# Graph message passing on one core: gathers released by message products, one wait for a quad's four one-hot columns, and bases loaded for eight quads at once

## The chip, the cores and the metric

The kernel runs on one core of one Trainium2 chip. The metric is the device time of one execution in microseconds (us), shown as the median of several runs. One more execution is taken by the hardware profiler; its time stands beside its span, which is the time from the first to the last instruction. Engines are called by the names of the profile: PE is TensorE (matmul), DVE is VectorE, ACT is ScalarE, POOL is GpSimd and SP is SyncE; "PEld" is TensorE's weight load, and an engine's name with a "q" (DVEq) is its sequencer or its DMA queue.

## What is computed

400,000 edges, sorted by destination, carry messages between 12,500 nodes of 128 features; a small network of each edge's length weighs the message, the sums per destination go through two layers, and a layer norm closes it:

```python
rbf = exp(-(distances[:, None] - centers) ** 2 / (2.0 * width * width))        # 50 centers from 0 to 10
cut = 0.5 * (cos(pi * distances / CUTOFF) + 1.0) * (distances <= CUTOFF)       # CUTOFF = 10
W = (silu(rbf @ fw1 + fb1) @ fw2 + fb2) * cut[:, None]
messages = (h[src] @ pw + pb) * W
agg = segment_sum(messages, dst, num_segments=12500)
x = layernorm(x + h + (silu(agg @ mw1 + mb1) @ mw2 + mb2))                     # here h is x
```

Lengths run up to 56, so that an edge over 10 (cut is 0) adds nothing, and fewer than a fifth of the edges count.

## The kernel before

**Packing.** The edges come in seven chunks. For each chunk the kernel works out which edges are within the cutoff and packs their source, destination, length and cut closely together. The pieces of this packing (DVE, PE and a scatter on POOL's queue at L524) are put between the steps of the main loop; the last chunk is packed in the second half of the run.

**Table.** In the first 118 us PE also multiplies x by pw and adds pb; the result, `proj`, lies in DRAM, one row per node.

**Main loop.** The packed edges are taken in quads of 4 x 128 edges, 139 in all (q = 0 to 138). For each quad:

- `fetch` gathers 4 x 128 rows of `proj` with four indirect DMAs on POOL's queue (L1099), one of 21 buffers a quad, later fewer. All the buffers are named by what they are lent from: the tiles `quad`, and `x`.
- `basis` (ACT), `first` (PE, L1167, tile `ph`), `silu` (ACT, L1173) and `second` (PE, L1182 and L1185, a PSUM `bank`) work out W without the cut.
- `message` is one DVE product of 128 x 512: the gathered rows by that bank (L1201). It writes `msg`, or, from quad 66 on, in half of the quads, a buffer called `quad`.
- `place` writes the quad's four one-hot columns (DVE, L1214, tile `hot`, or `quad` in half of the quads from 66 on): column j has the cut of an edge at the place of its destination within a window, 56 to 128 wide. These operations are called columns below.
- `sum_up` multiplies on PE: four products msg^T x hot, each in two passes (L1235, PSUM tile `sums`).
- `add` adds the window to the table of all sums `aggT` on DVE (L1269). Where the window begins is a number in memory (`base_i`); DVE's sequencer loads it into a register, for two quads at a time in `bases_of` (L1244) or for one in `base_of` (L1255). From quad 69 on a quad has two windows and so two bases.

In the loop the order of a quad is: `message(q)`, parts of the packing and of the node layer, the gathers that are due, `second(q+2)`, `first` and `silu` of another pair of quads, `sum_up(q)`, loads of bases, `place(q+1)`, and `add` of the two quads before. From quad 70 on the node layer (L1283 and the lines behind it) begins for the rows of `aggT` that are complete.

**Buffers.** `msg` and `hot` have two buffers each before quad 66 and four from then on, so `place(q+1)` writes into the buffer that the products of quad q-1 read: until those are through, the column has to wait.

**When a gather goes.** A table written out by hand, `PACE`, says at which count of DVE instructions (of the kinds in `VECTORS`) a gather is to go; `pace(q, j)` interpolates in it. `gathers` puts a gather on POOL's queue once that many DVE instructions have been written, and `fetch` adds a dependency: the gather waits for exactly that DVE instruction.

```python
    while queue and (queue[0][0] < must or len(vectors) >= pace(*queue[0])):
        ...
            g.ins, vectors[min(pace(q, j), len(vectors)) - 1],
```

The instructions of one engine run in the order in which they are written. The waits are semaphores that a framework puts in from what each instruction reads and writes. In the rows of instructions below, `PE_49`, `DVE_49` and so on are the semaphores that the named engine counts up, `DMASW0_49` to `DMASW7_49` those of POOL's DMAs.

Of the kernel before, what the change touches and what calls it, by code (L numbers as in the profile page):

```python
# [16 lines left out]
OP = mybir.AluOpType  # L17
# [9 lines left out]
W = 128  # L27
WIDE_0 = 128
WIDTHS = (56, 56, 80, 112, 80, 104, 128)
QT = 4  # L30
# [9 lines left out]
QB = (0, 13, 24, 46, 69, 91, 114, 141)  # L40
# [3 lines left out]
NL = 139  # L44
# [13 lines left out]
DIRECT = 32  # L58
FIRST = 16
LISTS = 5  # L60
PACE = ((2, 17), (3, 26), (4, 36), (5, 54), (7, 95), (9, 125), (10, 144), (12, 170), (18, 250), (24, 324), (30, 373), (36, 458), (42, 544), (48, 612), (54, 691), (60, 754), (66, 826), (72, 902), (78, 982), (84, 1071), (90, 1139), (96, 1218), (102, 1306), (108, 1357), (114, 1414), (120, 1461), (126, 1518), (132, 1580), (138, 1646), (139, 1666))
VECTORS = ("TensorScalarPtr", "TensorTensor", "CopyPredicated", "TensorReduce", "TensorCopy",
           "BNStats")
SPILL = 4
# [27 lines left out]
def kernel(  # L92
# [37 lines left out]
    nc = tc.nc  # L130
# [14 lines left out]
    keep = ctx.enter_context(tc.tile_pool(name="keep", bufs=1))  # L145
# [291 lines left out]

        return max((m for m in range(q) if place_of(m) == place_of(q)), default=-1)

    vectors, queue = [], []  # L440

    def logged(i):

# [5 lines left out]
    def pace(q, j):  # L449

        (a, u), (b, v) = next((k for k in zip(PACE, PACE[1:]) if q < k[1][0]))
        n = int(u + (v - u) * (q + j / QT - a) / (b - a))
        return n - sum(1 for w in WERE if w < q - 2)

    def gathers(must=0):

        while queue and (queue[0][0] < must or len(vectors) >= pace(*queue[0])):
            q, j = queue.pop(0)
            fetch(q, js=(j,))

    def room(q):

# [369 lines left out]
    def unpack(c):  # L832
# [66 lines left out]
        def back(t):  # L899
            held.remove(c)  # L900
            free.append(t)
# [19 lines left out]
        def to_places(f, to):  # L921
            t, tp = turned()
            for j in range(2):
                nc.tensor.transpose(tp[:, j, :np_], f[:, j * P:(j + 1) * P], ident[:np_, :np_])
            if to is srci:
                lengths()
                yield 1.4 if c < 2 else 0.8
            if to is dl:
                nc.tensor.matmul(tp[0:1, 0, P:P + np_], base, ident[:np_, :np_], start=True, stop=True)
            yield later(-2.0 if c == 1 and to is srci else 0.0)  # L930
            nc.vector.tensor_copy(to[:, p0:p0 + np_, :].rearrange("p r j -> p j r"),
                                  tp[:, :, :np_])
            if to is dl:
                nc.vector.tensor_copy(base_i[:, p0:p0 + np_], tp[0:1, 0, P:P + np_])
            back(t)

        yield from to_places(f_src, srci)
# [102 lines left out]
            own_sb[name, k] = keep.tile([P, QT, H], F32, name=f"{name}{k}")  # L1040
        return own_sb[name, k]

    own_sb = {}
# [49 lines left out]
    def fetch(q, idx=None, table=None, js=range(QT)):  # L1093
        got = quad_sb[place_of(q) if q >= 0 else 0]
        for j in js:
            if q in SINGLY and j == 0:
                continue
            i = srci[:, 2 * q + j // 2, j % 2:j % 2 + 1] if idx is None else idx[:, j:j + 1]
            g = nc.gpsimd.indirect_dma_start(  # L1099
                out=got[:, j, :], out_offset=None, in_=proj if table is None else table,  # L1100
                in_offset=bass.IndirectOffsetOnAxis(ap=i, axis=0))
            if PACE[0][0] <= q < NL:
                tc.add_manual_dep(
                    g.ins, vectors[min(pace(q, j), len(vectors)) - 1],
                    mybir.DependencyInfo(mybir.DependencyClass.Sync, mybir.DependencyReason.DATA))
        got_of[q] = got

# [81 lines left out]
    def message(q, js=(0, QT)):  # L1189
        gathers(q + 1)  # L1190
        msg = own(q, "msg", 0)
        a, b = js
        if q in SINGLY and a == 0:
            act = q in BY_ACT
            k = (BY_ACT if act else BY_SP).index(q)
            assert q in alone and all(s[0] != q for s in singles[act])
            nc.vector.wait_ge(row_sem[act][k % ROW_SEMS], 16 * P * (k // ROW_SEMS + 1))
            m = nc.vector.tensor_mul(msg[:, 0, :], pu_of[q][:, :H], alone.pop(q))
            tc.declare_no_dep(m.ins, group="rows", reason="waits on row_sem")
            a = 1  # L1200
        nc.vector.tensor_mul(msg[:, a:b, :], pu_of[q].rearrange("p (j f) -> p j f", j=QT)[:, a:b, :],  # L1201
                             got_of[q][:, a:b, :])
        if b == QT:
            free.append(pu_of.pop(q))
            got_of.pop(q)
        gathers()
        return msg

    def place(q):

        hot = own(q, "hot", 1)
        for j in range(QT):
            at = 2 * q + j // 2, slice(j % 2, j % 2 + 1)
            nc.vector.tensor_scalar(hot[:, j, :wide(q)], iota_n[:, :wide(q)], dl[:, at[0], at[1]],  # L1214
                                    cut[:, at[0], at[1]], op0=OP.is_equal, op1=OP.mult)
            gathers()
        hot_of[q] = hot

    def wide(q):

        return WIDE_0 if q < DIRECT // QT else WIDTHS[chunk_of(q)]

    def windows(q):

        return 1 if chunk_of(q) < WIDE_C else 2

    def sum_up(q, msg, js=range(QT)):
        hot = hot_of[q]
        if q % 2 == 0 and 0 in js:
            pa_of["two"] = ps.tile([P, 2, 2 * W], F32, name="sums", bufs=2)  # L1230
        pa = pa_of[q] = pa_of["two"][:, q % 2, :]
        n = QT // windows(q)
        for j in js:
            k = j // n
            nc.tensor.matmul(pa[:, k * W:k * W + wide(q)], msg[:, j, :], hot[:, j, :wide(q)],  # L1235
                             start=(j % n == 0), stop=(j % n == n - 1))

    bases = {}

    def bases_of(quads_now):  # L1240

# [9 lines left out]
    def base_of(q, ks=(0, 1)):  # L1251
        for k in ks:
            if k == windows(q):
                break
            _, v = nc.values_load_multi_w_load_instructions(  # L1255
                base_i[0:1, 2 * q + k:2 * q + k + 1], engines=[mybir.EngineType.DVE],
                min_val=0, max_val=N - wide(q),
                skip_runtime_bounds_check_because="bases are destinations, and end in the table")
            bases[q, k] = v[0]
# [333 lines left out]
    for q in range(NL - 7):  # L1593
        while todo and q + 2 >= DIRECT // QT and todo[0] <= chunk_of(min(q + 2, NQ - 1)):
            go_on(todo[0])
        msg = message(q)
        nodes(q)
        most[0] = room(q)
        fetches(clock[0], most[0])
        fetches(math.inf, min(NL, q + AHEAD + 1))  # L1600
        gathers()
        assert fetched[0] > QT * min(NL - 1, q + AHEAD)
        if q >= CLEAR_Q:
            clear()
        if loads_later and q >= 8:
            nc.sync.dma_start(*loads_later.pop(0))
        radials(q // 2 + 5)
        one_by_one()
        multiplies(q + 1 + EARLY_X)
        if q + 2 < NL:  # L1610
            second(q + 2)
        if q % 4 < 2 and 2 * octs(q) < NL:
            first(octs(q))
            silu(octs(q))
        if q % 4 == 3:
            for o in (q // 4 * 2 + 4, q // 4 * 2 + 5):
# [278 lines left out]
```

## Time and profile before

| | before |
|---|---|
| runs | 941.9, 945.89 and 944.31 us, median 944.31 |
| profiled execution | 950.38 us, span 948.8 us |
| mean granted TensorE clock | 0.808 |
| PE busy | 663.7 us (70%), 3531 instructions |
| PEld busy | 517.3 us (55%), 3531 |
| DVE busy | 565.9 us (60%), 1725 |
| ACT busy | 398.0 us (42%), 567 |
| POOL busy | 539.2 us (57%), 577 |

The busy time of an engine is the sum over its instructions, so none of the engines is busy all the time. Where the profile says `A <- B`, an instruction A of this engine stood idle until B released it; "remote" is a semaphore that came without a cause in the profile's records of that time, "issue" is idle time in which the engine waited for nothing that the profile shows.

### The profile page before, as it was taken

Reading aid. Unit: us, or ns where it says so; the run is one execution under the profiler, and the core shown is the slowest. Engines: PE = TensorE matmul, PEld = TensorE weight load, DVE = VectorE, ACT = ScalarE, POOL = GpSimd, SP = SyncE. Lnnn points to the kernel's source line nnn. Section 1 sums busy time; section 2 is a strip of 40 time slices with the busy share of each in tenths; the row PEclk is TensorE's granted clock in tenths of the full one; section 3 lists DMA queues with packets and bytes.
Section 4 is the critical chain, followed back from the end, with each engine's and each line's share of the span. In section 5 each row is a group of like instructions: output and inputs, shape, how many; then the busy total and the mean of one; then the engine's idle time right before and its main releaser. Section 6 shows DMA issues by size and latency. Waiting matters only on the chain.

```text
span 948.8 us, 11718 instructions
## 1 busy us (share of the span) xinstructions
PE 663.7 (70%) x3531; PEld 517.3 (55%) x3531; DVE 565.9 (60%) x1725; ACT 398.0 (42%) x567; POOL 539.2 (57%) x577
## 2 busy tenths in 40 slices
PE   4663737749778867767767786868796675777656
PEld 3552535537556755655555564646575554554444
DVE  8356638745778767767678584646553344443536
ACT  4432622316335443534334433634643542454235
POOL 6346355565556656666666465546565566664661
PEclk8677767778778878888978898769987787778778
DMA  7574421232233223232324122432422342232222
GB/s 243 161 222 154 147 96 34 77 92 81 62 79 120 71 62 82 69 108 77 94 64 136 54 68 67 120 100 67 142 63 63 105 122 67 65 111 81 70 75 74
DMA packets 51295, 91.23 MB, mean 96 GB/s; under 512 B 12928, under 2 KB 18656, under 8 KB 51226
## 3 DMA queue, kind: packets, MB, share of 16 engines
q0 software_dynamic: 18096, 37.30, 15.6%
q1 hardware_dynamic: 22868, 35.09, 11.2%
q10 hardware_dynamic: 10262, 18.05, 6.0%
q8 instruction: 29, 0.48, 0.2%
q14 instruction: 40, 0.33, 0.1%
HBM read 74.59 MB, written 15.79 MB: 95 GB/s over the span
## 4 chain that ended last, share of the span: by engine, by line
PE 42%; another core or an unknown queue 16%; issue 13%; DVE 13%; ACT 10%; DVEq 1%; DMA 1%; ACTq 0%
PE ph L1167 11%; PE bank L1185 9%; PE sums L1235 9%; PE bank L348 5%; DVE hot L1214 3%; PE bank L1182 3%; PE bank L1283 2%; DVE msg L1201 2%; ACT s L1173 2%; ACT rbf L1151 2%; PE bank L1003 1%; PE bank L345 1%; ACT rbf L1155 1%; DVE aggT L1269 1%
## 5 line engine op out<-in xcount | busy, mean ns | idle before, releaser
L1099 POOL DMA_INDIRECT quad<-proj,srci x412 | 391.7, 951 | 274.0 <-issue 86.1
L1185 PEld LDWEIGHTS bank<-fw_sb,s 128*128 128x128 f32 x1112 | 177.1, 225 | 90.2 <-issue 83.6
L1173 ACT ACTIVATE s<-ph 128x1024 f32<-128x1024 f32 x70 | 71.2, 1017 | 335.6 <-PE ph L1167 159.9
L1167 PE MATMUL ph<-rbf,w_sb 102*128 102x512 f32 x278 | 164.1, 719 | 51.7 <-ACT s L1173 35.7
L1185 PE MATMUL bank<-fw_sb,s 128*128 128x128 f32 x1112 | 180.1, 310 | 22.5 <-issue 22.2
L1214 DVE TENSOR_SCALAR hot<-iota_n,dl,cut 128x80 f32<-128x80 f32 (+4 forms) x408 | 111.1, 338 | 107.0 <-PE sums L1235 49.6
L1235 PEld LDWEIGHTS sums<-hot,msg 128*128 128x128 f32 x816 | 121.5, 218 | 61.3 <-issue 40.3
L1235 PE MATMUL sums<-hot,msg 128*128 128x80 f32 (+4 forms) x816 | 122.5, 299 | 17.3 <-DVE msg L1201 10.1
L1099 POOL DMA_INDIRECT x<-proj,srci x96 | 91.4, 952 | 66.4 <-issue 21.3
L1167 PEld LDWEIGHTS ph<-rbf,w_sb 102*128 102x128 f32 x278 | 57.3, 229 | 99.7 <-issue 58.8
L1269 DVE TENSOR_TENSOR aggT<-aggT,sums 128x80 f32 (+4 forms) x209 | 53.9, 258 | 94.1 <-remote 33.8
L1182 PE MATMUL bank<-fb_b,ones_b 96*128 96x512 bf16 x139 | 60.3, 434 | 49.6 <-DVE msg L1201 15.2
L1201 DVE TENSOR_TENSOR msg<-bank,quad 128x512 f32<-128x512 f32 x78 | 53.2, 682 | 46.2 <-remote 32.7
L348 PEld LDWEIGHTS bank<-pw_sb,xT 128*128 128x128 f32 (+1 forms) x292 | 47.2, 232 | 59.0 <-issue 40.3
L1099 POOL DMA_INDIRECT quad<-in_x_dram,srci x48 | 46.3, 965 | 33.9 <-issue 12.6
L1235 PE MATMUL sums<-quad,quad 128*128 128x128 f32 (+3 forms) x296 | 49.4, 309 | 15.8 <-issue 15.2
L1151 ACT ACTIVATE rbf<-d_sb,rbf_bias,rbf_scale 102x512 f32<-102x512 f32 x70 | 56.1, 801 | 0.0
L1235 PEld LDWEIGHTS sums<-quad,quad 128*128 128x128 f32 x296 | 45.0, 225 | 20.1 <-issue 18.8
L348 PE MATMUL bank<-pw_sb,xT 128*128 128x128 f32 (+1 forms) x292 | 48.5, 319 | 6.2 <-ACT xT L1005 5.6
L345 PE MATMUL bank<-pb_b,ones_b 96*128 96x512 bf16 (+2 forms) x38 | 16.8, 443 | 46.4 <-ACT xT L1005 29.0
L1201 DVE TENSOR_TENSOR quad<-bank,quad 128x512 f32<-128x512 f32 (+1 forms) x40 | 25.9, 647 | 38.0 <-DMA quad<-proj,srci 24.2
L1005 ACT COPY xT<-bank 128x512 f32<-128x512 f32 (+1 forms) x37 | 21.3, 580 | 63.5 <-remote 49.0
(278 smaller groups left out, 881.7 us busy)
## 6 DMA issues: line engine op xcount, KB each, us to landing
d_sb<-near_d ACTq DMA_DIRECT2D x67, 256.0 KB
x<-in_x_dram SPq DMA_DIRECT2D x46, 256.0 KB
quad<-proj,srci POOLq DMA_INDIRECT x412
proj<-hp SPq DMA_DIRECT2D x24, 256.0 KB
out_dram<-x SPq DMA_DIRECT2D x22, 256.0 KB
x<-proj,srci POOLq DMA_INDIRECT x96
r_d<-in_edge_weight_dram SPq DMA_DIRECT2D x5, 256.0 KB
r_dst<-in_dst_dram SPq DMA_DIRECT2D x5, 256.0 KB
```

What stands on the lines that cost most here:

```text
L345: nc.tensor.matmul(to[:m, a:a + c, :], ones_b[:, :m], bias_b[:, :c, :], start=True, stop=False)
L348: nc.tensor.matmul(to[:m, k, :], lT[:, k * P:k * P + m], w, start=False, stop=(k == a + c - 1))
L1099: g = nc.gpsimd.indirect_dma_start(out=got[:, j, :], out_offset=None, in_=proj if table is None else table, in_offset=bass.IndirectOffsetO ...
L1151: a = nc.scalar.activation(rbf[:u], d[:u], AF.Square, bias=rbf_bias[:u], scale=rbf_scale[:u])
L1167: nc.tensor.matmul(ph[:, h, :], w1_sb[:2 * KR, h, :], rbf[:2 * KR], start=True, stop=True)
L1173: nc.scalar.activation(s[:, :n], ph[:, :n], AF.Silu)
L1182: nc.tensor.matmul(pu, ones_b[:, :P], bias_b["fb2"].rearrange("k j f -> k (j f)"), start=True, stop=False)
L1185: nc.tensor.matmul(pu[:, j * H:(j + 1) * H], s[:, j * P:(j + 1) * P], fw2_sb, start=False, stop=(j == QT - 1))
L1201: nc.vector.tensor_mul(msg[:, a:b, :], pu_of[q].rearrange("p (j f) -> p j f", j=QT)[:, a:b, :], got_of[q][:, a:b, :])
L1214: nc.vector.tensor_scalar(hot[:, j, :wide(q)], iota_n[:, :wide(q)], dl[:, at[0], at[1]], cut[:, at[0], at[1]], op0=OP.is_equal, op1=OP.mult)
L1235: nc.tensor.matmul(pa[:, k * W:k * W + wide(q)], msg[:, j, :], hot[:, j, :wide(q)], start=(j % n == 0), stop=(j % n == n - 1))
L1269: nc.vector.tensor_add(to, to, pa[:, k * W:k * W + wide(q)])
```

## The change

It has three parts. Gathers: `products` keeps the count of DVE instructions at each message product. A gather is put on the queue at the first message product whose count is at least its pace less `HALF` (6), at the latest when the pace plus 6 is reached, and waits for that message product in place of any DVE instruction. Columns: of a quad's four columns only the first has a dependency on the products that read the buffer before, and it is on the last of them; the other three have none. Bases: `bases_of` loads up to eight quads' bases in one instruction, as far as the windows are of one width and number and their bases are there; what is loaded isn't loaded again.

```diff
+HALF = 6
+BASES = 8
 def gathers(must=0):
-        while queue and (queue[0][0] < must or len(vectors) >= pace(*queue[0])):
+        while queue and (queue[0][0] < must or products[-1:] >= [pace(*queue[0]) - HALF]
+                         or len(vectors) >= pace(*queue[0]) + HALF):
             q, j = queue.pop(0)
             fetch(q, js=(j,))
+    def tied_to(q, j):
+        n = pace(q, j) - HALF
+        return vectors[next((k for k in products if k >= n), products[-1]) - 1]
...
             if to is dl:
                 nc.vector.tensor_copy(base_i[:, p0:p0 + np_], tp[0:1, 0, P:P + np_])
+                with_base[0] = QB[c + 1]
...
-            if PACE[0][0] <= q < NL:
+            if PACE[0][0] <= q < NL and products:
                 tc.add_manual_dep(
-                    g.ins, vectors[min(pace(q, j), len(vectors)) - 1],
+                    g.ins, tied_to(q, j),
...
             got_of.pop(q)
+            products.append(len(vectors))
...
-            nc.vector.tensor_scalar(hot[:, j, :wide(q)], iota_n[:, :wide(q)], dl[:, at[0], at[1]],
-                                    cut[:, at[0], at[1]], op0=OP.is_equal, op1=OP.mult)
+            i = nc.vector.tensor_scalar(hot[:, j, :wide(q)], iota_n[:, :wide(q)], dl[:, at[0], at[1]],
+                                        cut[:, at[0], at[1]], op0=OP.is_equal, op1=OP.mult).ins
+            if id(hot) in read_by:
+                tc.declare_no_dep(i, group="sums", keep=[read_by[id(hot)]] if j == 0 else [],
+                                  reason="a quad's first column waits for the last product")
+                if j == 0:
+                    tc.add_manual_dep(i, read_by[id(hot)].name, mybir.DependencyInfo(
+                        mybir.DependencyClass.Sync, mybir.DependencyReason.DATA))
...
-            nc.tensor.matmul(pa[:, k * W:k * W + wide(q)], msg[:, j, :], hot[:, j, :wide(q)],
-                             start=(j % n == 0), stop=(j % n == n - 1))
+            i = nc.tensor.matmul(pa[:, k * W:k * W + wide(q)], msg[:, j, :], hot[:, j, :wide(q)],
+                                 start=(j % n == 0), stop=(j % n == n - 1)).ins
+            if not tc.in_control_flow:
+                tc.add_to_no_dep_group("sums", i)
+                read_by[id(hot)] = i
...
             if k == windows(q):
                 break
+            if (q, k) in bases:
+                continue
...
         if at_once:
-            bases_of(list(now))
+            ahead = list(now)
+            while (len(ahead) < BASES and ahead[-1] + 1 < min(with_base[0], NL - 7)
+                   and wide(ahead[-1] + 1) == wide(now[0])
+                   and windows(ahead[-1] + 1) == windows(now[0])):
+                ahead.append(ahead[-1] + 1)
+            if any((k, 0) not in bases for k in now):
+                bases_of([k for k in ahead if (k, 0) not in bases])
```

What this does to the engines' instructions is seen at two places. The first is DVE around quads 14 and 15, before:

```order
L1201 TENSOR_TENSOR msg0_1078<-bank0_167,x41_87 128x512 [waits DMASW4_49,DMASW5_49,DMASW3_49,DMASW2_49]
L1214 TENSOR_SCALAR hot1_1111<-iota_n_145,dl_158,cut_157 128x56 [waits PE_49] x4
L931 COPY cut_157<-bank2_169 128x2x44
L549 SCALAR_TENSOR_TENSOR nodes_1783<-bank3_170,nodes_1729 128x512 [waits DVE_49]
L1201 TENSOR_TENSOR msg1_680<-bank1_168,x42_88 128x512 [waits DMASW6_49,DMASW7_49,DMASW1_49,DMASW0_49]
L1244 TENSOR_LOAD base_i_159 [waits DVE_49]
L1214 TENSOR_SCALAR hot0_1073<-iota_n_145,dl_158,cut_157 128x56 [waits PE_49] x4
L1269 ISA
L1269 TENSOR_TENSOR aggT_99<-aggT_99,sums_1715 128x56
```

The same place on DVE in the changed kernel (its line numbers are higher by some 10 to 20):

```order
L1210 TENSOR_TENSOR msg0_1078<-bank0_167,x41_87 128x512 [waits DMASW4_49,DMASW5_49,DMASW3_49,DMASW2_49]
L1224 TENSOR_SCALAR hot1_1111<-iota_n_145,dl_158,cut_157 128x56 [waits PE_49]
L1224 TENSOR_SCALAR hot1_1111<-iota_n_145,dl_158,cut_157 128x56 x3
L939 COPY cut_157<-bank2_169 128x2x44
L557 SCALAR_TENSOR_TENSOR nodes_1787<-bank3_170,nodes_1738 128x512 [waits DVE_49]
L1210 TENSOR_TENSOR msg1_680<-bank1_168,x42_88 128x512 [waits DMASW6_49,DMASW7_49,DMASW1_49,DMASW0_49]
L1224 TENSOR_SCALAR hot0_1073<-iota_n_145,dl_158,cut_157 128x56 [waits PE_49]
L1224 TENSOR_SCALAR hot0_1073<-iota_n_145,dl_158,cut_157 128x56 x3
L1290 ISA
L1290 TENSOR_TENSOR aggT_99<-aggT_99,sums_1724 128x56
```

The order is the same; three of four columns have lost their wait on PE, and the load of bases between product and columns is gone here (quad 11 has loaded those of quads 8 to 15). From quad 66 on no column waits for PE in either kernel. Over the whole program DVE has 24 loads of bases in place of 82, with 1 to 16 registers each, and 62 columns wait on PE in place of 248; the instructions of PE that count a semaphore up fall from 601 to 393.

The second place is POOL's queue at the gathers of quads 113 and 114, before:

```order
L1099 DMA quad9_82<-proj,srci_156 128x128 [waits DMASW3_49,DVE_49]
L1099 DMA quad9_82<-proj,srci_156 128x128 [waits DMASW4_49,DVE_49]
L1099 DMA quad9_82<-proj,srci_156 128x128 [waits DMASW5_49,DVE_49]
L1099 DMA quad9_82<-proj,srci_156 128x128 [waits DMASW6_49,DVE_49]
L1099 DMA quad10_83<-proj,srci_156 128x128 [waits DMASW7_49,DVE_49]
L1099 DMA quad10_83<-proj,srci_156 128x128 [waits DMASW0_49,DVE_49]
L1099 DMA quad10_83<-proj,srci_156 128x128 [waits DMASW1_49,DVE_49]
L1099 DMA quad10_83<-proj,srci_156 128x128 [waits DMASW2_49,DVE_49]
```

The same gathers in the changed kernel:

```order
L1108 DMA quad9_82<-proj,srci_156 128x128 [waits DMASW3_49]
L1108 DMA quad9_82<-proj,srci_156 128x128 [waits DMASW4_49]
L1108 DMA quad9_82<-proj,srci_156 128x128 [waits DMASW5_49,DVE_49]
L1108 DMA quad9_82<-proj,srci_156 128x128 [waits DMASW6_49]
L1108 DMA quad10_83<-proj,srci_156 128x128 [waits DMASW7_49]
L1108 DMA quad10_83<-proj,srci_156 128x128 [waits DMASW0_49]
L1108 DMA quad10_83<-proj,srci_156 128x128 [waits DMASW1_49,DVE_49]
L1108 DMA quad10_83<-proj,srci_156 128x128 [waits DMASW2_49]
```

Before, each gather waits for a DVE instruction of its own; now the third of a quad's gathers waits for a message product here, and the next three go with it. The gathers' own order is kept; only beside the scatters of L524 a few of them change places by one to three.

More of the change, by code (lines that the diff above doesn't have):

```diff
@@ L438, in before_it @@
         return max((m for m in range(q) if place_of(m) == place_of(q)), default=-1)
-    vectors, queue = [], []
+    vectors, queue, products = [], [], []
     def logged(i):
@@ L1041, in own @@
         return own_sb[name, k]
-    own_sb = {}
+    own_sb, read_by = {}, {}
     singles, alone, regs, row_at = ([], []), {}, {}, [0.0]
@@ L1234, in sum_up @@
             k = j // n
-            nc.tensor.matmul(pa[:, k * W:k * W + wide(q)], msg[:, j, :], hot[:, j, :wide(q)],
-                             start=(j % n == 0), stop=(j % n == n - 1))
-    bases = {}
+            i = nc.tensor.matmul(pa[:, k * W:k * W + wide(q)], msg[:, j, :], hot[:, j, :wide(q)],
[3 more added lines that the diff above has]
+                read_by[id(hot)] = i
+    bases, with_base = {}, [DIRECT // QT]
     def bases_of(quads_now):
```

## The prediction

> **What bounds the kernel now.** I read the page first, for a leader among the engines.
>
> ```profile
> span 948.8 us, 11718 instructions
> ...
> PE 663.7 (70%) x3531; PEld 517.3 (55%) x3531; DVE 565.9 (60%) x1725; ACT 398.0 (42%) x567; POOL 539.2 (57%) x577
> ...
> PE 42%; another core or an unknown queue 16%; issue 13%; DVE 13%; ACT 10%; DVEq 1%; DMA 1%; ACTq 0%
> ```
>
> None is above 70%, and the chain that ended last is mostly PE; its second share, 16% or 152 us, is signals that came late without a recorded cause. On one core "another core" can only be a queue or a semaphore that was slow. So each stage has to be read by who waits in it. The windows cut the run at quad 66 (499 us), from which columns no longer wait for PE, and at 700 us.
>
> ```profile
> core 0: us, PE busy (x) PEld busy (x) DVE busy (x) ACT busy (x) POOL busy (x), PEclk, DMA share, GB/s
> 130.00:499.00 369.00, 266.63 (x1388) 209.21 (x1388) 251.45 (x677) 143.55 (x178) 219.10 (x231) 0.80 0.28 76
> 499.00:700.00 201.00, 154.53 (x832) 117.92 (x831) 120.78 (x402) 95.14 (x133) 114.01 (x120) 0.85 0.33 93
> 700.00:949.00 249.00, 171.68 (x895) 130.48 (x894) 114.06 (x392) 105.07 (x159) 138.28 (x147) 0.81 0.28 82
> ```
>
> DVE is busy 68% of the first of these stretches and 46% of the last. Its waits in 130 to 499 us, and then in 499 to 949 us:
>
> ```profile
> DVE hot L1214 <- PE sums L1235: 49.6, 18, 14.6
> DVE hot L1214 <- remote: 44.9, 18, 5.3
> ...
> DVE aggT L1269 <- remote: 33.8, 7, 6.7
> DVE msg L1201 <- remote: 30.9, 5, 8.3
> DVE quad L1201 <- DMA quad<-proj,srci: 24.2, 10, 4.8
> DVE quad L1201 <- remote: 10.0, 3, 6.2
> DVE msg L1201 <- DMA quad<-proj,srci: 7.8, 4, 2.3
> ```
>
> In the first stretch 94.5 of DVE's 117.6 idle us stand ahead of the columns: the change touches the very wait that holds DVE there. In the second it touches only the gathers, which hold a message 14 times, 32.0 us together.
>
> **The columns.** Two kinds of waits are in those 94.5 us; DVE's timeline shows both.
>
> ```profile
> 429.94 1.08 DVE L1214 TENSOR_SCALAR hot<-iota_n,dl,cut 128x112 f32<-128x112 f32 x4 [3.75 <-remote]
> ...
> 171.35 0.34 DVE L1214 TENSOR_SCALAR hot<-iota_n,dl,cut 128x128 f32<-128x128 f32 x1 [0.35 <-PE bank L1003]
> ...
> 466.86 0.34 DVE L1214 TENSOR_SCALAR hot<-iota_n,dl,cut 128x112 f32<-128x112 f32 x1 [1.63 <-PE sums L1235]
> 468.96 0.34 DVE L1214 TENSOR_SCALAR hot<-iota_n,dl,cut 128x112 f32<-128x112 f32 x1 [1.76 <-remote]
> 471.06 0.34 DVE L1214 TENSOR_SCALAR hot<-iota_n,dl,cut 128x112 f32<-128x112 f32 x1 [1.76 <-remote]
> 471.79 0.34 DVE L1214 TENSOR_SCALAR hot<-iota_n,dl,cut 128x112 f32<-128x112 f32 x1 [0.40 <-remote]
> ```
>
> In the first row all four columns run in one piece: (1.08 - 0.34) / 3 = 0.25 us from one start to the next. There are 19 such places up to 499 us. The last product's signal was there at most 3 x 0.25 = 0.74 us after the first one's, or the fourth column would have stood alone. Waiting for it at the first column therefore costs 0 to 0.74 us, together 0 to 14.
>
> In ten other quads the signals came one by one: 17 rows like the last three, from 171.35 to 471.79 us, show 18.8 us of idle time between a quad's columns. Now the first column starts when the last signal comes, where the fourth starts today, and the other three follow: if the last signal comes as now, each of the ten loses 0.74 us, 7.4 together. If it comes as early as the first one does now, all 18.8 us are gone. So the columns are worth -18.8 to +21.4.
>
> Which? The steps in the last four rows are 2.10, 2.10 and 0.73 us, though the products themselves are short:
>
> ```profile
> L1235 PE MATMUL sums<-hot,msg x816: 209/275/554, 145.4 to 936.3; 128*128 128x80 f32 x52, 128*128 128x112 f32 x34, 128*128 128x128 f32 x33, 128*128 128x56 f32 x26
> L1235 PE MATMUL sums<-quad,quad x296: 229/275/539, 506.1 to 939.8; 128*128 128x128 f32 x52, 128*128 128x80 f32 x44, 128*128 128x104 f32 x44, 128*128 128x112 f32 x8
> ```
>
> By PE's records the products were over long before ("remote"), so signals are late, which speaks for a gain by fewer of them. Against it: "remote" waits do not thin out from 499 us on, where no column waits for PE (33.8 + 30.9 + 10.0 us there in three rows alone, 44.9 at the columns before). The rows point both ways between ends that lie almost evenly about nothing; I take 0 and keep both ends. What hides a small loss here is the next late signal of PE: DVE comes to it 0.7 us later and waits 0.7 us less.
>
> [...]
>
> Behind the first column stand, on DVE, the other three, the two sums into aggT, the packing's steps and the next message product; for that product's `msg` and these columns wait PE's next products, and now also the gathers tied to it. All of it moves by what the column moves.
>
> **The gathers.** POOL's rows:
>
> ```profile
> L1099 POOL DMA_INDIRECT quad<-proj,srci x412: 938/944/1322, 104.7 to 930.2; - x138
> ...
> 708.64 0.94 POOL L1099 DMA_INDIRECT quad<-proj,srci  x1 [0.30 <-issue]
> 709.89 0.94 POOL L1099 DMA_INDIRECT quad<-proj,srci  x1 [0.30 <-issue]
> ```
>
> A gather holds POOL 0.944 us and the next starts 0.30 us behind it, although each has a wait on DVE of its own; 1.25 us each, 5.0 us for four. Taking waits away makes this no shorter: nothing. What moves is when a gather may start. The four of a quad were released over the quad's 9 to 15 DVE instructions; now about four are released at one message product, some earlier than their count and some later (the tie is the first product from count - 6 on). For a mean distance of 12 between products that is 6 earlier to 6 later, on average nothing; but four released together run 5.0 us, so the last of them starts 3.75 us behind its release.
>
> Before 499 us DVE never waits for a gather (no such row), so nothing comes of it there. Behind 700 us it does. I replayed POOL's queue with DVE's times held: each gather starts at the later of its new release plus the usual 0.3 us and the end of the gather ahead plus 0.30. Late gathers come 0.5 to 1 us later on average, two quads (105 and 117) nearly 5, with their messages 1.6 and 1.9 us later; over the waits for gathers that is about +3.5 us. It could also be -2 (gathers released earlier that today wait for their count) or +10 (the same delay at each of the 14 waits). Behind 700 us a message that is late is partly covered by late PE work: I take +2.
>
> **The loads of bases.** They run in DVE's sequencer, between product and columns.
>
> ```profile
> L1244 DVEq TENSOR_LOAD <-base_i x32: 508/512/757, 161.0 to 497.4; - x32
> L1244 DVEq TENSOR_LOAD <-base_i x28: 337/344/686, 509.4 to 845.5; - x28
> L1244 DVEq TENSOR_LOAD <-base_i x1: 1333/1333/1333, 901.3 to 901.3; - x1
> L1201 DVE TENSOR_TENSOR msg<-bank,quad x78: 665/681/698, 120.9 to 934.1; 128x512 f32<-128x512 f32 x78
> 902.71 1.12 DVE L1214 TENSOR_SCALAR hot<-iota_n,dl,cut 128x128 f32<-128x128 f32 x4 [0.57 <-issue]
>   issue: 5.9, 10
> ```
>
> The three groups are loads of 2 registers with a stride, of 4 in a row and one of 14 in a row. The message product of 0.68 us covers loads of 0.51 and 0.34 us; columns stand idle by "issue" 5.9 us in the whole run (last row, of the view of L1214), 0.57 of it behind the one load that is longer than a product, of 14 registers. So removing 58 loads saves at most 5.9 - 0.57 = 5.3 us, likely 3.5. The new ones are longer: 16 registers in a row take about 1.33 + 2 x (1.33 - 0.34) / 10 = 1.5 us and stick out 0.85 us; 8 with a stride 0.51 + 6 x 0.10 = 1.1 to 4 x 0.51 = 2.0 us, 0.4 to 1.4 beyond the product. Eight strided and seven or so long ones cost 9 to 17 us if nothing covered them; the strided ones lie ahead of columns that wait for PE in 29 quads of 64 anyway. From -5 to +12; I take -1.
>
> **Columns beside gathers.** A gather released by the message product starts on top of the columns that follow.
>
> ```profile
> L1214 DVE TENSOR_SCALAR hot<-iota_n,dl,cut x408: 275/328/569, 117.8 to 931.8; 128x80 f32<-128x80 f32 x44, 128x112 f32<-128x112 f32 x28, 128x128 f32<-128x128 f32 x27, 128x56 f32<-128x56 f32 x21
> ```
>
> The longest column is 0.24 us over the median; today some columns end beside a gather and are held by up to that. If one more column in 20 to 60 quads is held by 0.1 us or less, that is 0 to +5 us on DVE, less on the path; I take 0.
>
> **Sum:** 0 + 2 - 1 + 0 = +1 us on the profiled execution's 950.38. That execution lies 6.1 us above the median of the runs (944.31), so I forecast 945.3, said as 945.
>
> **Rivals.** What this kernel can tell from no change is about 0.5%, 4.7 us: 939.6 to 949.0.
>
> *A, late signals are PE's own making (faster).* If fewer signals let the last one come where the first comes now, the ten trickling quads give back up to 18.8 us, and a part of the 44.9 us of "remote" goes too. For it: the 2.10 us steps while PE's records have moved on. Against it: the "remote" rows from 499 us on. With two thirds of the 18.8 on the path, 933.
>
> *B, pacing or loads help (faster).* POOL idles until a DVE instruction of its own count; earlier releases take some of that away, and 58 loads less take away 5.3 us. With -2 for gathers and -5 for loads, 938.
>
> *C, the last product costs (slower).* If signals come as now, the 29 quads lose 7.4 + up to 14 us, of which DVE's chain before 499 us passes most on: it decides when DVE rather than PE is late at the columns. With two thirds of 21, +14: 958. It decides from about 0.3 us a quad on.
>
> *D, bursts are late behind 700 us (slower).* If each of the 14 gather-bound messages loses 0.6 to 0.7 us and a few more join them, +9: 953.
>
> *E, an engine blocks the other (slower).* If columns and gathers that now start together excluded each other, each of some 120 quads would lose up to a column, 0.33 us, or +40: 984. The row above speaks against it, since no column is held longer than 0.24 us and gathers are 944 ns nearly always. [...]
>
> *F, nothing that counts changes,* because waits removed were never the last to come: the forecast's own neighbour, counted with it.
>
> **How the numbers follow.** My forecast, with F: 0.34, own range 939 to 950. A 0.22, B 0.15, C 0.18, D 0.09, E 0.02. Faster by over 0.5% is A and B, 0.37; slower C, D and E, 0.29. The range runs from about all of the columns' gain (944.3 - 18.8 = 925.5) to C with a part of D (944.3 + 18 = 962): 926 to 962. Outside lie A with more than the gaps between columns, E, and C with all of D, together under 2 in 10.
>
> **What would show it.** Columns: rows of single columns vanish; right if DVE's sum of waits at the first column in 130 to 499 us stays at 94.5 - 18.8 + 11 = 85 to 105 us; if it falls below 70, A holds; if quad 66 comes over 5 us later, C. Gathers: message waits on gathers of 30 to 38 us; over 42 is D, under 25 B. Loads: columns idle by "issue" 5 to 12 us. Wrong altogether, if the "remote" rows from 499 us on also change by tens of us: then what makes signals late was touched, which none of my terms prices.

## The result: 6.5% slower, by the gathers' part

The changed kernel takes 1006.96 us (median of four runs, 998.6 to 1011.69) against 944.67 us of the kernel before (941.9 to 945.89): a ratio of 1.065, interval 1.058 to 1.073. Its profiled execution takes 1011.69 us. Here and below, an execution over 1.5% above the fastest of its kernel is left out of ratios and their intervals, and where this leaves too few, no ratio is given. These lines of its page answer to those of before:

```profile
span 1010.1 us, 11317 instructions
...
PE 678.6 (67%) x3531; PEld 522.6 (52%) x3531; DVE 562.5 (56%) x1725; ACT 398.5 (39%) x567; POOL 539.4 (53%) x577
...
PE 25%; DVE 13%; another core or an unknown queue 13%; issue 12%; POOL 5%; ACT 4%; DMA 1%; DVEq 1%; POOLq 0%; ACTq 0%
```

No engine has more instructions to run than before. DVE and POOL are busy within 4 us of before; PE is busy 15 us longer, at a lower granted clock (0.789 in place of 0.808). Beyond that, the 61 us are idle time. POOL has turned up in the chain that ended last.

The windows are cut at quad 66 again, which now begins at 559 us:

```profile
core 0: us, PE busy (x) PEld busy (x) DVE busy (x) ACT busy (x) POOL busy (x), PEclk, DMA share, GB/s
130.00:559.00 429.00, 273.71 (x1406) 211.25 (x1404) 253.67 (x687) 144.49 (x180) 233.37 (x245) 0.77 0.23 68
559.00:1010.00 451.00, 327.26 (x1685) 246.42 (x1685) 229.68 (x783) 197.14 (x287) 249.42 (x263) 0.81 0.28 86
```

Up to quad 66 nearly the same DVE work (253.7 us; 255.2 before, from 130 us to the start of quad 66's message at 505.3 us) fills 429 us in place of 375. Behind it, the changed kernel needs 451 us and the kernel before 444 (505 to 949). The message product of quad 66 in the two timelines, first before, then after:

```profile
505.33 0.69 DVE L1201 TENSOR_TENSOR quad<-bank,quad 128x512 f32<-128x512 f32 x1
...
559.23 0.69 DVE L1210 TENSOR_TENSOR quad<-bank,quad 128x512 f32<-128x512 f32 x1
```

So 54 of the 61 us are lost before quad 66, where no message waits for a gather. DVE's waits over the whole run, of the changed kernel:

```profile
DVE hot L1224 <- remote: 68.8, 12, 9.8
DVE aggT L1290 <- remote: 48.5, 8, 10.8
DVE hot L1224 <- PE sums L1251: 47.4, 13, 15.5
DVE msg L1210 <- remote: 41.5, 8, 9.0
DVE msg L1210 <- DMA quad<-proj,srci: 19.6, 8, 4.0
DVE hot L1224 <- issue: 15.5, 11, 9.8
DVE quad L1210 <- DMA quad<-proj,srci: 14.9, 7, 3.7
```

The rows with "remote", DVE's waits for signals that came without a recorded cause (PE's late signals, by the next section), add up to 191 us over all lines, against 139 before: 52 us more. The waits of messages for gathers hardly move: 34.5 us in 15 waits, 32.0 in 14 before.

What POOL does differently is seen best at the start of the loop. Its timeline, changed kernel, at the first gathers from `proj` and at the end of their run:

```profile
98.96 0.94 POOL L1108 DMA_INDIRECT quad<-in_x_dram,srci  x1 [0.30 <-issue]
123.77 0.95 POOL L1108 DMA_INDIRECT quad<-proj,srci  x1 [23.87 <-DVE msg L1210]
125.02 0.95 POOL L1108 DMA_INDIRECT quad<-proj,srci  x1 [0.30 <-issue]
...
150.00 0.94 POOL L1108 DMA_INDIRECT x<-proj,srci  x1 [0.30 <-issue]
159.71 0.94 POOL L1108 DMA_INDIRECT x<-proj,srci  x1 [8.77 <-DVE msg L1210]
```

POOL stands idle for 24 us until the very first message product, and then sends 22 gathers without a break, in the loop's first quads. Before, the first 21 gathers began at 104.7 us, while the table was still being made, had a break of 3.2 us among them, and ended here:

```profile
133.62 0.94 POOL L1099 DMA_INDIRECT x<-proj,srci  x1 [0.30 <-issue]
147.21 0.95 POOL L1099 DMA_INDIRECT x<-proj,srci  x1 [12.64 <-DVE base_i L934]
```

### The profile page after: what moved, and what is told of

It is laid out like the page before. It is cut to its first block, busy times and chain, and to the rows that moved or that the text cites. A ratio compares the mean times of both kernels' runs of the same rounds, so it can differ in the third digit from the quotient of the medians.

```text
span 1010.1 us, 11317 instructions
## 1 busy us (share of the span) xinstructions
PE 678.6 (67%) x3531; PEld 522.6 (52%) x3531; DVE 562.5 (56%) x1725; ACT 398.5 (39%) x567; POOL 539.4 (53%) x577
## 4 chain that ended last, share of the span: by engine, by line
PE 25%; DVE 13%; another core or an unknown queue 13%; issue 12%; POOL 5%; ACT 4%; DMA 1%; DVEq 1%; POOLq 0%; ACTq 0%
PE ph L1176 8%; PE bank L1194 6%; PE sums L1251 6%; POOL quad L1108 5%; DVE hot L1224 3%; DVE msg L1210 2%; PE bank L1304 2%; PE bank L1191 2%; PE bank L350 1%; DVE aggT L1290 1%; ACT s L1182 1%; DMA quad<-proj,srci 1%; DVE quad L1224 1%; DVE bank L553 1%
## 5 line engine op out<-in xcount | busy, mean ns | idle before, releaser
L1176 PE MATMUL ph<-rbf,w_sb 102*128 102x512 f32 x278 | 168.2, 732 | 44.8 <-ACT s L1182 30.4
L1224 DVE TENSOR_SCALAR hot<-iota_n,dl,cut 128x80 f32<-128x80 f32 (+4 forms) x408 | 108.4, 335 | 151.2 <-remote 68.8
L1251 PE MATMUL sums<-hot,msg 128*128 128x80 f32 (+4 forms) x816 | 125.4, 301 | 29.4 <-issue 17.2
L1306 ACT ACTIVATE zs<-bank 128x512 f32<-128x512 f32 (+2 forms) x27 | 15.0, 555 | 84.6 <-remote 36.9
L1182 ACT ACT_TABLE_LOAD x35 | 44.9, 1283 | 0.8 <-issue 0.2
```

The costliest lines, as they stand in the source:

```text
L1176: nc.tensor.matmul(ph[:, h, :], w1_sb[:2 * KR, h, :], rbf[:2 * KR], start=True, stop=True)
L1182: nc.scalar.activation(s[:, :n], ph[:, :n], AF.Silu)
L1224: i = nc.vector.tensor_scalar(hot[:, j, :wide(q)], iota_n[:, :wide(q)], dl[:, at[0], at[1]], cut[:, at[0], at[1]], op0=OP.is_equal, op1=OP ...
L1251: i = nc.tensor.matmul(pa[:, k * W:k * W + wide(q)], msg[:, j, :], hot[:, j, :wide(q)], start=(j % n == 0), stop=(j % n == n - 1)).ins
```

## What a run of gathers does to PE's signals

This reading of the traces gave the theory that the experiments test. PE's signals can be matched, in order, with the ends of the PE instructions that send them; a signal's lateness is its recorded time less that end. The profile models these ends, so a product that ended later than modelled would look the same as a late signal. I sorted the signals by how long gathers had then been running without a break of 0.5 us, over eleven profiles with late signals (behind 118 us, 3039 signals):

| gathers running without a break for | signals | mean lateness, us | over 0.4 us late |
|---|---|---|---|
| not running | 714 | 0.08 | 7% |
| 0 to 2.5 us | 871 | 0.32 | 14% |
| 2.5 to 5 us | 483 | 0.56 | 23% |
| 5 to 7.5 us | 444 | 1.56 | 66% |
| 7.5 to 10 us | 276 | 2.19 | 81% |
| 10 to 12.5 us | 174 | 2.76 | 95% |

Another 77 signals lie behind 12.5 us, 2.3 us late and more on average. Signals that come more than about 5 us behind any end that is still unmatched stay out of the table, so the means of the long runs are low: matched up to 15 us, the rows rise from 0.1 to between 5 and 6 us. PE's signals are mostly on time beside no gather or a short run, and fall behind as a run goes on. In the kernel before, the part from 118 to 560 us has 271 gathers from `proj` in 62 runs; in the changed kernel 246 in 38. Theory L: the change makes the runs longer, and the later signals hold DVE and ACT. Rival C: the single wait at the first column costs. Rival P: it is the start right behind a message product, together with the columns.

## The experiments

**The change in its parts.** One part at a time, and the change without its gathers' part. Each result stands against the kernel before on the same chip. In what was expected of these four, theory G is that the gathers' part is the cause, by whatever way.

> Only the columns' part: the first column waits for the last sum product, the other three for nothing; gathers and loads of bases as before. Theory C (the single wait at the first column makes the columns late wherever signals of PE come late, and each place passes it on): most of the 62 us, 985 to 1010 us. Theory G (the gathers' new release is the cause): the columns are about neutral as predicted, 935 to 955 us.

> Only the gathers' part: they are released by message products; columns and loads of bases as before. Theory G: most of the 62 us, 985 to 1010 us, lost before quad 66. Theory C: 940 to 958 us, what is lost being lost behind 700 us, where messages wait for gathers.

> Only the bases' part: up to eight quads' bases in one load. Both theories: 939 to 950 us, since the loads lie beside the message product but for some tenths of a microsecond each. A time over 960 would say that the long loads themselves hold the columns.

> Columns and bases together, gathers as before, that is the changed kernel without its gathers' part. Theory C: as the changed kernel, 990 to 1012 us. Theory G: as the kernel before, 935 to 955 us. If each part alone is near the kernel before and this one too, the loss needs the gathers together with another part.

| kernel | median us | before, same chip | ratio |
|---|---|---|---|
| only_columns | 967.5 (946.5 to 969.9) | 954.9 | none |
| only_gathers | 1010.2 | 954.9 | 1.046 (1.033 to 1.058) |
| only_bases | 950.9 | 954.9 | 0.997 (0.992 to 1.002) |
| no_gathers | 955.8 (943.0 to 966.1) | 954.9 | none |

The ratio of `only_gathers` rests on two of its four runs, 995.8 and 1009.2 us; the medians would give 1.058. The gathers' part alone gives most of the loss, and these runs do not tell whether all of it; its rows of DVE's waits:

```profile
DVE hot L1222 <- remote: 97.1, 35, 9.8
DVE aggT L1277 <- remote: 74.2, 12, 9.8
DVE msg L1208 <- remote: 38.1, 7, 8.2
```

That the other two parts cost nothing together was settled by a second run of `no_gathers`, with more executions:

> Columns and bases without the gathers' part, as the version that could beat both kernels. Where PE's signals are late: within 1% of the kernel before, as measured. Where they are not and POOL's gathers set the pace (some 737 us): within 0.5%, since neither columns nor loads are waited for by POOL; a ratio under 0.995 would say that the loads that went did count there.

Measured: 942.5 against 942.4 us, 1.002 (0.997 to 1.006). Columns and bases are neutral, and rival C falls: the version without the gathers' part equals the kernel before and doesn't beat it.

**Four at a time, but not at message products.** In the kernel before, `pace` is rounded:

```diff
-        return n - sum(1 for w in WERE if w < q - 2)
+        return round((n - sum(1 for w in WERE if w < q - 2)) / 12) * 12
```

> The kernel before with each gather's pace rounded to the nearest multiple of 12 DVE instructions: gathers are released about four at a time as in the change, but by any DVE instruction and not at message products; columns and loads as before. Theory L (PE's signals come later the longer gathers follow one another without a break: in the traces so far 0.1 us late with no gather running, 0.5 us in the first 5 us of an unbroken run, 1.5 us behind that and 3 us behind 10 us): 970 to 1010 us. Rival P (it is the start beside the columns, right behind a message product, that costs): 940 to 955 us.

Measured: 976.5 against 954.4 us, 1.024 (1.017 to 1.030). This is what theory L expects in kind: 259 gathers in 31 runs between 118 and 560 us, "remote" 184 us. It is a third of the changed kernel's loss, so that bursts alone, without the change's first run, do not account for all of it. Nor does the length of runs set the loss by itself: from the first message product to that of quad 66, gathers run beyond the first 5 us of a run for 118 us in the kernel before, 152 in the changed one and 155 here, where quad 66 comes 17 us later in place of 54.

**Pauses between gathers.** In the changed kernel:

```diff
+            if 12 <= q < OWN_4:
+                nc.gpsimd.memset(pause, 0.0)
             g = nc.gpsimd.indirect_dma_start(
```

> The changed kernel with a memset of 128 x 128 on POOL (about 0.2 us) ahead of each gather of quads 12 to 65, so that gathers come at most every 1.45 to 1.5 us. Theory L: runs of gathers leave PE's signals time, faster than the changed kernel: 960 to 995 us. Rival W (gathers and what is queued behind them come too late in the changed kernel): the pauses make them later still, 1005 to 1030 us.

Measured: 994.9 against 954.4 us, 1.041 (1.033 to 1.049), below the changed kernel's interval though each gather of quads 12 to 65 has a memset ahead of it (one of this size takes 204 ns in the kernel before). Rival W falls. The time is at the upper end of what L expected, and its mechanism is not seen here: DVE's "remote" rows add up to 185.5 us, in place of 191.3 in the changed kernel.

**The gathers below quad 24.** These are the first run and those that follow it. The changed kernel with the gathers of quads below 24 released and tied as before:

```diff
+KEPT = 24
-        while queue and (queue[0][0] < must or products[-1:] >= [pace(*queue[0]) - HALF] ...
+        while queue and (queue[0][0] < must or (
+                len(vectors) >= pace(*queue[0]) if queue[0][0] < KEPT else ...
+        if q < KEPT:
+            return vectors[min(pace(q, j), len(vectors)) - 1]
```

> The changed kernel with the gathers of quads below 24 released and tied as before. In the trace of the changed kernel the first 22 gathers from proj run without a break from 123.8 to 151 us, in place of 104 to 134 us, and quads 0 to 24 lose some 27 of the 62 us. Theory E (that one long run, pushed from the table's time into the loop's first quads, costs some 20 to 27 us by itself): 980 to 992 us on the scale where the changed kernel takes 1007. If the loss follows from bursts in every quad alike: 998 to 1010 us.

> The changed kernel with the gathers of quads below 24 as before, once more. Where PE's signals are late and the kernel before takes 940 to 960 us: theory E says a ratio of 1.03 to 1.045 in place of the changed kernel's 1.065; bursts alike in every quad say 1.055 or more. Where it takes some 737 us: 1.002 to 1.007, as measured twice, against 1.014 of the changed kernel.

The first of these runs fell on another kind of chip (below). In the second, `early_kept3`, 980.2 against 942.4 us: 1.046 (1.040 to 1.052) in place of 1.065, about 18 us back, just short of the 20 expected. The start of the message products, us, shows where:

| quad | before | by_12 | early_kept3 | changed |
|---|---|---|---|---|
| 9 | 221.5 | 218.1 | 222.0 | 244.4 |
| 24 | 293.1 | 296.2 | 295.2 | 320.7 |
| 66 | 505.3 | 522.1 | 527.0 | 559.2 |
| 138 | 936.0 | 957.4 | 961.0 | 996.8 |

Up to quad 24 the changed kernel loses 27.6 us, 22.9 of them by quad 9, and `early_kept3` 2.2: that part comes with the gathers below quad 24. From there to quad 66 they lose 26 and 20 us, `by_12` 14; behind it little (7, 3 and 5 us). So about 25 us go with these gathers (the first run alone was not put back), and some 20 to 26 with the releases at message products before quad 66, of which 14 come with any releases by twelves. These are single profiles: `only_bases`, a neutral kernel, reaches quad 24 at 296.2 us and quad 66 at 510.0, so that steps of 5 us say little. The rest of 6 to 12 us was not taken apart.

**Half of the gathers.** The kernel before, third and fourth gather left out from quad 24 on:

```diff
-            if q in SINGLY and j == 0:
+            if q in SINGLY and j == 0 or 24 <= q < NL and j > 1:
                 continue
```

> The kernel before without the third and fourth gather of each quad from quad 24 on (those messages are made of old rows): runs of gathers are half as long. Theory L: 860 to 915 us, most of the late signals of PE gone behind 290 us. If gathers cost only where a message waits for one: 915 to 935 us (32 us of such waits in the kernel before).

Measured: 720.3 against 954.4 us, 0.756 (0.750 to 0.761): 234 us less, far below what L had expected, and seven times what messages had waited for gathers. Not all of it need be late signals: on chips without any, `busy_pool` (below) has memsets in place of the same gathers and gains 33 us. The three "remote" rows that are left in DVE's waits:

```profile
DVE msg L1201 <- remote: 6.5, 3, 3.2
DVE turned_d L677 <- remote: 3.9, 1, 3.9
DVE hot L1214 <- remote: 1.8, 1, 1.8
```

The granted clock changes with it: 0.83 up to the message of quad 24 at 266 us, 0.96 and more behind it, and PE is busy 580 us in place of 664. How much of the gain is this clock was not separated from the late signals, nor which of the two follows from the other.

**The same gathers with an eighth of the bytes.** Rows of 64 B in place of 512 B:

```diff
-                out=got[:, j, :], out_offset=None, in_=proj if table is None else table,
+                out=got[:, j, :16] if 24 <= q < NL else got[:, j, :], out_offset=None,
+                in_=proj.rearrange("n (a f) -> (n a) f", f=16) if 24 <= q < NL else ...
```

> The kernel before with gathers of 64 B a row in place of 512 B from quad 24 on (the messages behind it are made of wrong rows): POOL issues the same gathers with the same number of rows, with an eighth of the bytes. If the bytes that gathers move make PE's signals late: 880 to 920 us, and few waits for late signals behind 290 us. If it is the gathers' number of rows or POOL's work on them: 935 to 950 us, waits as before.

Measured: 955.5 against 954.4 us, 0.999 (0.994 to 1.003), "remote" 121 us in place of 139. The time is 5 us above the range for rows or POOL's work, because the kernel before was slower here too. The bytes are not the cause; the gathers are, by their number, their rows or POOL's work on them.

**Chips without late signals.** Two sets of runs fell on chips where the kernel before takes 735.7 to 737.4 us. The runs there:

> The changed kernel with its gathers tied to a quad's fourth column in place of its message product: as many at a time, some 2 us later in the quad, no longer started together with the columns. Theory L (long runs alone): 998 to 1012 us. Theory P (the start right behind the message product adds to it): 965 to 990 us.

> The changed kernel itself once more. If the kernel before takes 940 to 960 us in this run, with waits for late signals of PE: 1000 to 1025 us, as first measured. If it takes some 737 us, without such waits, as in the runs just before: what the gathers' part costs by late signals is gone, and only POOL's later gathers are left: 738 to 750 us.

> The changed kernel with the gathers of quads below 24 as before, again. Where the kernel before takes 940 to 960 us: theory E (the first long run of gathers, moved into the loop's first quads, costs 20 to 27 us by itself) says 20 to 27 us below the changed kernel; bursts alike in every quad say at most 8 below. Where it takes 737 us: 739 us, as already measured.

> The kernel before with 64 rows in place of 128 in each gather from quad 24 on (half of each message is made of old rows): as many gathers, half the rows. If what a gather does to the others goes by its rows: 760 to 880 us, as without half of the gathers. If it goes by the gather as an instruction: 930 to 950 us.

> The kernel before with 64 rows in each gather from quad 24 on, again. A gather of 64 rows takes 0.90 us, one of 128 rows 0.94 us, so that POOL is as busy as before. Where the kernel before takes 940 to 960 us: if signals are late by a gather's rows, 740 to 850 us; if by the gather as an instruction, 920 to 950 us. Where it takes 737 us: 716 us, as already measured.

> The kernel without the third and fourth gather of each quad from quad 24 on (720 us), with two memsets of 128 x 512 on POOL, about 1.1 us, in the place of each (those messages are made of old rows). If POOL being at work is what makes PE's signals late: 900 to 950 us. If it is what gathers send out: 715 to 760 us.

> Two gathers of each quad from 24 on replaced by two memsets each on POOL, again. Where the kernel before takes 940 to 960 us: POOL at work as such as the cause says 900 to 950 us, what gathers send out says 715 to 760 us. Where it takes 737 us: 704 us, as already measured.

`at_fourth_column` puts `products.append(len(vectors))` behind a quad's fourth column; `half_rows` gives `[:64]` to a gather's target and indices; `busy_pool` has two memsets where `half_gathers` leaves a gather out.

| kernel | median us | before, same chip | ratio |
|---|---|---|---|
| changed_again | 747.3 | 735.7 | 1.014 (1.012 to 1.016) |
| early_kept | 738.8 | 737.4 | 1.002 (1.000 to 1.004) |
| early_kept2 | 739.2 | 735.7 | 1.005 (1.002 to 1.007) |
| at_fourth_column | 745.0 | 737.4 | 1.010 (1.007 to 1.012) |
| half_rows, half_rows2 | 716.0, 716.0 | 737.4, 735.7 | 0.971 (0.968 to 0.973), 0.974 (0.971 to 0.976) |
| busy_pool, busy_pool2 | 704.0, 705.0 | 737.4, 735.7 | 0.955 (0.952 to 0.959), 0.959 (0.955 to 0.963) |

The changed kernel costs 1.4% there, not 6.5%. Lines of its page and DVE's longest waits on such a chip:

```profile
span 747.1 us, 11317 instructions
...
POOL 18%; DVE 17%; DMA 17%; issue 14%; PE 10%; DVEq 1%; ACT 0%; POOLq 0%; ACTq 0%
...
DVE msg L1210 <- DMA quad<-proj,srci: 54.4, 25, 4.9
DVE quad L1210 <- DMA quad<-proj,srci: 44.2, 20, 4.8
DVE hot L1224 <- PE sums L1251: 24.8, 15, 4.7
```

There is no "remote" row at all. POOL sends gathers almost without a break, one each 1.25 to 1.29 us from 400 to 410 us with 0.30 us between them, and sets the pace: its 18% is the largest share of the chain that ended last; 45 messages wait for a gather, 98.6 us together. What is left of the loss, 11.5 us, goes for the most part with the gathers below quad 24, ahead of which POOL is idle in the changed kernel (busy 4 tenths of the time from 75 to 93 us, 7 in `early_kept`), since `early_kept` and `early_kept2` win back 8 to 10 of it. That the same long runs do no harm here says that a run of gathers is not enough by itself: the loss of 6.5% came where PE's signals fall behind, and 1.4% is lost where they don't. Theory P stays untried where it mattered, and so does whether the rows, the instruction or POOL's work makes the signals late: `at_fourth_column`, `half_rows` and `busy_pool` had no late signals to take away.

## Why the prediction was wrong

The step that failed is "Before 499 us DVE never waits for a gather (no such row), so nothing comes of it there". The reading is right, and in the changed kernel too no message waits for a gather before quad 66; but 54 of the 61 us are lost there. The step priced gathers only by the messages that wait for them, and took the wait rows of DVE as the whole of what a gather does. By that narrow measure it was right: those waits were forecast at 30 to 38 us and are 34.5. But in these profiles PE's signals come late where gathers run, by 2.8 us on average at 10 to 12.5 us of a run: with half of the gathers gone, DVE's late waits fall from 139 to 12 us and the time by 234 us. The gathers' term was given as +2 with -2 to +10. The whole change measured +62 us; its other two parts measure 1.002 together, and the gathers' part alone 1.046 (1.033 to 1.058). That the loss comes by the length of runs, and not also by their place behind a message product or by the clock, is argued and not shown.

- **"Remote" had no price.** The prediction saw 16% of the chain, and some 120 us of DVE's waits in the rows that it shows, come late without a cause, and asked only whether fewer signals of PE would mend it. The question that would have helped is what runs while a signal is late; the table of lateness could have been made from the trace of before. The last test that it named looked at these rows from quad 66 on, where they rise by 16 us only (88 to 104); the larger rise, 51 to 87 us, is ahead of it. And quad 66, which comes 54 us later, would have been read as rival C by the prediction's own sign, wrongly.
- **The first run was overlooked.** The replay looked at late gathers behind 700 us. It did not ask what the first run of 22 gathers, moved by 19 us, would then lie beside. With the gathers below quad 24 go 25 us, and 8 to 10 us even where signals are on time.
- **Bursts of four were seen, and only half followed.** "four released together run 5.0 us" is right, and at 5 us the lateness jumps from 0.56 to 1.56 us; the prediction asked only for the last gather of the four.
- **Columns: right, at nothing.** The two parts without the gathers measure 1.002, and the two waits at the columns, 94.5 us before, are 48.6 + 44.9 us in `no_gathers`. That the term is nothing was a middle between -18.8 and +21.4 that the rows left open, so the number is partly luck. In the changed kernel the two waits are 68.8 + 47.4 us, which looks like rival C, but a rise as large comes with the gathers alone (97.1 + 32.2).
- **Loads: right in size.** The columns' idle time by "issue" is 18.1 us, above the 5 to 12 named, but one wait of 9.8 us is over half of it and no load is that long. The sequencer's row of the changed kernel's longer loads, for 1.1 to 2.0 us forecast:

```profile
L1263 DVEq TENSOR_LOAD <-base_i x19: 341/1389/2078, 170.4 to 958.8; - x19
```

- **Rival D had the sign, not the place:** it put bursts behind 700 us, where gathers bind messages. **Rival E** falls: the columns are 292/328/586 ns against 275/328/569, and gathers 938/944/1316 ns. Columns that lie beside no gather take 346 ns at most before and 345 now; the longest that meet one, 569 and 586 ns, are some 0.24 us longer, which is far less than the 0.94 us of a gather.

## What to carry to other kernels

An engine's transfers can cost time that no one's wait for them shows: of the 62 us lost here, 2.5 are waits of messages for gathers. Where a trace has late signals without a cause, sort them by what else was running, and for how long without a break, before any of it is moved. When releases are tied to coarser events, ask for the first and the longest run that this makes and what it then lies beside, not only for the lead of the last transfer. And measure a change of this kind on more than one chip: here the same two kernels are 6.5% and 1.4% apart.

## What was not expected of the hardware

The same kernel takes 942 to 955 us on two of the four chips that ran the experiments, and 736 to 737 us on the other two. Gathers take the same time on both kinds, 944 and 947 ns. Two things differ.

The first is PE's signals. On the slower chips they fall behind during runs of gathers, by 2.8 us at 10 to 12.5 us; on the others they are 0.01 us late in every class of the table. The difference begins ahead of the loop, where gathers run too: the first gather from `proj` starts at 104.7 us in the kernel before on a slower chip, and at 71.8 us on a faster one in `half_rows`, which has the same gathers below quad 24.

The second is the granted clock, 0.80 to 0.82 in profiles of the kernel and its near relatives on the slower chips and 0.90 to 0.92 on the faster ones. It is no fixed property of the chip, since `half_gathers` has 0.96 and more behind quad 24 on a slower one. That chip then runs the kernel in 720 us, so it is not slow in itself.

The records differ as well. On the slower chips, in the eleven profiles of the table, at least 47 to 108 of PE's 393 to 601 signals have no record of their own, nor have 364 to 532 of DVE's and 138 to 186 of ACT's; the recorded signals of DVE and ACT are less than 0.1 us late on average. On the faster chips at most 3 of an engine lack one. `half_gathers` lacks 83, 288 and 95, though from quad 24 on it hardly waits for late signals, so missing records go with the chip and not with the time lost.

Every time of this case has a recorded span and clock beside it, so whether signals are late when nothing is recorded, and why chips differ, stays open.
